# A CIN kernel on one core: block 1's first two tiles by plain transfers, the order of TensorE's first products, and the queues of the two output transfers

## The chip, the cores and the metric

The kernel runs on one core of a Trainium2 chip. The metric is the device time of one execution in microseconds (us). The core has five engines that run side by side and wait for each other by semaphores: TensorE (PE in the profile; its weight loads are PEld), VectorE (DVE), ScalarE (ACT), GpSimd (POOL) and SyncE (SP). Transfers are issued by SyncE, ScalarE or GpSimd, each with a queue of its own, and moved by the core's 16 DMA engines.

## What is computed

Three layers of a compressed interaction network for 1024 samples, each with 39 fields of 64 numbers, and a last linear layer on the sums of all three:

```python
def _cin_layer(Xk, X0, W, b):
    O = W.shape[0]
    Hk, Fdim = (Xk.shape[1], X0.shape[1])
    Wr = W.reshape(O, Hk, Fdim)
    return jnp.einsum('bhe,bfe,ohf->boe', Xk, X0, Wr) + b[None, :, None]
X0 = sparse_embedding            # 1024 x 39 x 64
Xk = X0
outs = []
for W, b in ((W0, b0), (W1, b1), (W2, b2)):   # 64 outputs each
    Xk = _cin_layer(Xk, X0, W, b)
    outs.append(Xk.sum(axis=-1))
cin_output = jnp.concatenate(outs, axis=-1)
return cin_output @ fc_w.T + fc_b
```

## The kernel before

**What it makes of the reference.** Layers 2 and 3 and the final layer are linear in their inputs apart from the products with X0, so the kernel folds W2, W1 and fc into a few small matrices during a preparation, and is left with the products of pairs of fields (layer 1's input) times weights, and one more multiplication per sample. The products of all pairs of 39 fields and a constant one are gathered in such a way that VectorE multiplies whole tiles of 128 rows, and TensorE multiplies the result by weights.

**Blocks and tiles.** The samples are cut into blocks of 32 (2048 columns). For a block, `rt` holds five tiles of 128 rows and 2048 columns of fp32 (8 KB a row). Each row is one field of the block, in an order that `label(i, row)` gives for tile i. `PAIRS` names six pairs of tiles; `product(n, c)` on VectorE is the product of one pair (the first one is tiles 0 and 1), and a seventh small one is made from `ut` and `vt`, for two blocks at a time. TensorE (`multiply`, L551) multiplies each product in four quarters of 512 columns. `rt` has two buffers: block 0 uses the first, block 1 the second.

**How the rows come.** The fields of a block are brought from the input into a table in DRAM, `xd`, with one row of 8 KB per field (`load`, L140), and are then spread over the 128 rows of each tile: `roll` issues one gather for each tile on GpSimd (L147), with row numbers from `lists`. Block 0's first four tiles are gathered in halves out of another table, `xh`, to be early. Later blocks (L719 and L763, most of the time) work in a different form, on tables `wc` and `wn`, with products made by L736.

**The preparation.** The names that matter here are: `fcrow2`, parts of fc doubled on GpSimd; `turn`, a product of one row that turns it into a column (L306); `spin`, fillers on TensorE that compute nothing of use (L259, into `idle`); V2, which is W2 with fc folded in (L386, then VectorE's transposes L406); `spread_v2` (L420, then VectorE's L433), which spreads it to both halves of the partitions; `turn_w0`, seven transposes of W0 (L399), read by ScalarE's copies L444; V1, which is W1 with V2 folded in (L467, then VectorE's transposes L480 and copies L487 and L490 into `both`); `weight_rows` (L508 and L510), which puts together the weights of one product in `pairs`; and `weight_turn`, which transposes them on TensorE (L527) and copies them into `wa` on ScalarE (L528). The order of the instructions on each engine is written out by hand.

**The order after that.** Block 0's first three products are made in halves, then the others; TensorE takes them in their order, block 0's seven, then block 1's six, and so on. VectorE makes a product four steps ahead of TensorE. On SyncE's queue stand, in order: fc's row, two copies of `xh` into `xd` (L376), the ones of the next table (L349), and the loads of blocks 2 and 3, and of 4 and 5. On GpSimd's queue stand block 0's gathers, u's and v's, block 1's five gathers, some small vectors, and then block 2's gathers.

**The end.** `finish_quarter` sums up the last block. Three rows of 256 results go out by SyncE (L1081), the last row by ScalarE (L1091); a last part of 8 results is made by VectorE (L1090).

Of the kernel before, what the change touches and what calls it, by code (L numbers as in the profile page):

```python
# [11 lines left out]
ALU = mybir.AluOpType  # L12
AX = mybir.AxisListType

B, F, E, H = 1024, 39, 64, 64
FH = F * H
FT = F + 1
# [3 lines left out]
NT = 5  # L21
# [8 lines left out]
MM = 512  # L30
# [9 lines left out]
NTAB = 3  # L40
NY = 3
# [19 lines left out]
def label(i, row):  # L61
    if row < K:
        return (row % F + BASE[i] + STEP[i] * (row // F)) % F
    e = row - K
    if i == NT - 1 and e < ONLY:
        return F
    return 3 * e + (e >= ONLY) + (e > ONLY) + OFFSET[i]


def small_labels(r):  # L70
# [44 lines left out]
def cin_kernel(ctx: ExitStack, tc: tile.TileContext, x, w0t, b0, w1, b1, w2, b2, fc_w, fc_b, out):  # L115
    nc = tc.nc
# [10 lines left out]
    xd = [dram.tile([2 * FT, BLK], F32, name=f"xd{k}") for k in range(NTAB)]  # L127
# [5 lines left out]
    def behind(work, product):  # L133
        if product is not None:
            info = mybir.DependencyInfo(mybir.DependencyClass.Sync, mybir.DependencyReason.DATA)
            tc.add_manual_dep(work.ins, product.ins.name, info, reason="one transfer per product")
# [15 lines left out]
    def tiles_of(n):  # L152
        return rt[(n + (n // 2 == NPART - 1)) % 2]

    def roll(n, tiles=range(NT), product=None):
        for i in tiles:
            k = n % 2 * NT + i
            gather_rows(tiles_of(n)[:, i], xd[n // 2 % NTAB][: FT if k < NT else 2 * FT], k, product)

    def roll_small(n):  # L160
        table = xd[n // 2 % NTAB].rearrange("f (t c) -> (f t) c", c=SUB)
        for k, dst in enumerate((ut, vt)):
            gather_rows(dst[n // 2 % 2], table, 2 * NT + k)
# [4 lines left out]
    v2v = v2.rearrange("p (low s b) -> p low s b", s=2, b=32)  # L168
# [18 lines left out]
    ones = const.tile([16, 2, 128], F32, name="ones")  # L187
# [3 lines left out]
    pairs = const.tile([128, NCHUNK, 128], F32, name="pairs")  # L191
    unit = const.tile([128, 128], F32, name="unit")

    def product(n, c, cols=slice(0, BLK), p=None):
        if p is None:
            p = prods.tile([128, BLK], F32, name="p", tag="p")
        if c < NPAIR:
            i, k = PAIRS[c]
            r = tiles_of(n)
            nc.vector.tensor_tensor(p[:, cols], r[:, i, cols], r[:, k, cols], ALU.mult)  # L200
        else:
            nc.vector.tensor_tensor(p[:, 0:SUB], ut[n // 2 % 2], vt[n // 2 % 2], ALU.mult)
        return p

    prep = tc.tile_pool(name="prep", bufs=1)
    with prep as prep:
# [5 lines left out]
        fcrow2 = prep.tile([1, 2, H, 2], F32, name="fcrow2")  # L212
# [8 lines left out]
        mask = prep.tile([128, 2], F32, name="mask")  # L221
# [31 lines left out]
        pw = [bank("pw") for _ in range(2)]  # L253
        small = bank("small")


        def spin(n=1, cols=MM // 2):
            for _ in range(n):
                nc.tensor.matmul(  # L259
                    idle[:, 0:cols],  # L260
                    nc.const_aps.tensor(1.0, (128, 128), F32),
                    nc.const_aps.tensor(1.0, (128, cols), F32),
                    start=True,
                    stop=True,
                )
# [23 lines left out]
        row, j, f0, late, v, extra = (new() for _ in range(6))  # L289
# [3 lines left out]
        for i in range(NT):  # L293
            at = OFFSET[i] - 3 * K + (0 if i < NT - 1 else -F)
            for k, by in enumerate((STEP[i], BASE[i], at)):
                nc.gpsimd.memset(shifts[:, k, i : i + 1], float(by))
        for k, by in enumerate((*SHIFT, ROWS, *(ROWS + by for by in SHIFT[NK - 1 :]))):
            nc.gpsimd.memset(shift_of[:, k : k + 1], float(by))
        one = ones[0:1, 0, 0:1]

        def double(dst, src):
            for s in range(2):
# [2 lines left out]
        def turn(dst, row):  # L305
            nc.tensor.matmul(dst, row, one, start=True, stop=True)  # L306
# [1 line left out]
        def turn_row(h, at, row, k):  # L308
            turn(small[h : h + H, at : at + 1], row[:, k * H : k * H + H])

        def turn_twice(at, row, k):
            turn(small[:, at : at + 1], row[:, k].rearrange("p h s -> p (h s)"))

        double(fcrow2[:, 1], fcrow[:, 2 * H : 3 * H])
        double(fcrow2[:, 0], fcrow[:, H : 2 * H])
# [4 lines left out]
        bothv = both.rearrange("p (a b) -> p a b", b=FT)  # L320
        nc.gpsimd.memset(bothv[0:H, :, F], 0.0)
        first = pw[1][:, MM - 1 : MM]
        turn(first, fcrow2[:, 1].rearrange("p h s -> p (h s)"))
        spin(1, MM // 4)

        nc.vector.tensor_copy(row, place)
        step(row, F, 1.0, j)
# [32 lines left out]
        r, most, far = (new() for _ in range(3))  # L360
# [22 lines left out]
        for k in range(2):  # L383
            for u in range(2):
# [5 lines left out]
                    start=True,  # L390
                    stop=True,
                )

        turn_twice(6, fcrow2, 0)
        spin(1, 3 * MM // 8)

        def turn_w0(k):
            n = min(128, NF * H - k * 128)
            nc.tensor.transpose(  # L399
                pw[k // 4][0:n, k % 4 * NW * F : (k % 4 + 1) * NW * F],  # L400
                w0s[:, k * 128 : k * 128 + n],
                unit[0 : NW * F, 0 : NW * F],
            )

        for k in range(2):
# [1 line left out]
                blocks[:, k].rearrange("p (f h) -> p f h", h=32),  # L407
                pv[k][:, 0:320].rearrange("p (h f) -> p f h", f=10),
            )
        nc.vector.tensor_scalar(v2v[:, 0, :, F - 32], mask, small[:, 6:7], None, ALU.mult)  # L410
        nc.vector.tensor_tensor(steps_at, steps_at, steps_by, ALU.mult)
        fused(seat, row, 96.0, seat, ALU.is_ge, ALU.add)
        step(row, 64.0, 2.0 * FT - 1.0, far)
# [4 lines left out]
        def spread_v2(u, lo, n):  # L418
            rows = slice(H * u, H * u + H)
            nc.tensor.matmul(  # L420
                pv[u][:, 0:n],
                twice[rows].rearrange("p h s -> p (h s)"),
                column[rows, lo : lo + n],
                start=True,
                stop=True,
            )

        spread_v2(0, 0, 20)
        spread_v2(1, 1, 19)
        for k in range(7):  # L430
            turn_w0(k)
        for u, at, low, lo, n in ((0, 0, 1, 0, 20), (1, 0, 1, 20, 12), (1, 12, 0, 0, 7)):
            nc.vector.tensor_tensor(  # L433
                v2v[:, low, :, lo : lo + n],
# [17 lines left out]
        nc.vector.tensor_tensor(both_of[:, 1:2], both_of[:, 0:1], jumps[:, 1:2], ALU.add)  # L452
        nc.vector.tensor_scalar(lists[:, 2 * NT :], both_of, 2.0, seat, ALU.mult, ALU.add)
        roll_small(0)
        roll(1)
        for h in (0, H):
            nc.gpsimd.dma_start(b0s[h : h + H], b0.rearrange("(h o) -> h o", o=1))
        nc.gpsimd.dma_start(b1s, b1.rearrange("(h o) -> h o", o=1).to_broadcast([H, 2]))
# [7 lines left out]
        for k, a in groups:  # L466
# [4 lines left out]
                start=True,  # L471
                stop=True,
# [2 lines left out]
        for h in (0, H):  # L475
            turn_row(h, 1, fcrow, 0)
        turn_row(0, 2, fcrow, 2)
        spin(3)
        for k, a in groups:
            nc.vector.transpose(  # L480
                flat[:, k], pt[k][:, 0 : 32 * NA].rearrange("p (h f) -> p f h", f=NA)
# [1 line left out]
        for k, a in groups:  # L483
# [4 lines left out]
            if k > 1:  # L488
                first = slice(0, 3) if k == 2 else slice(k, k + 1)
# [6 lines left out]
        first = [prods.tile([128, BLK], F32, name="p", tag="p") for _ in range(3)]  # L496


    def weight_rows(c, some=slice(None)):
        for at, n, a, b, sa, sb in RUNS[c][some]:  # L500
            out = pairs[:, c, at : at + n]

            def diagonal(p, q, sp, sq):
                at, by = p * FT + q, sp * FT + sq
                return both[:, at : at + by * (n - 1) + 1 : by]

            if b == F or a == b:
                nc.scalar.copy(out, diagonal(a, b, sa, sb))  # L508
            else:
                nc.vector.tensor_tensor(  # L510
                    out, diagonal(a, b, sa, sb), diagonal(b, a, sb, sa), ALU.add
                )
# [18 lines left out]
    work = ctx.enter_context(tc.tile_pool(name="work", bufs=2))  # L531
# [359 lines left out]
    steps = []  # L891
# [13 lines left out]
    p = {}  # L905
# [16 lines left out]
    for at, (n, c) in enumerate(steps[:3]):  # L922
        if at < 2:
            weight_rows(steps[3][1], slice(6 * at, 6 + 6 * at))
        product(n, c, halves[1], p[n, c])
    weight_rows(steps[4][1])
    n, c = steps[3]
    p[n, c] = product(n, c, halves[0])
# [149 lines left out]
            stop=True,  # L1078
        )
    nc.scalar.activation(y, py[0 : NY * 32, 0:YB], AF.Identity, bias=kfin)  # L1080
    nc.sync.dma_start(outv[0:NY], y[0 : NY * 32 : 32])  # L1081
    for lo, hi in ((0, done), (done, YB)):
        py = bank("py")[0:1, 0 : hi - lo]
        nc.tensor.matmul(
# [3 lines left out]
            nc.scalar.activation(yl[:, lo:hi], py, AF.Identity, bias=kfin[0:1])  # L1088
        else:
            nc.vector.tensor_scalar(yl[:, lo:hi], py, kfin[0:1], None, ALU.add)  # L1090
    nc.scalar.dma_start(outv[NY : NY + 1], yl)  # L1091


# [40 lines left out]
```

## Time and profile before

| | us |
|---|---|
| median of three runs | 735.3 |
| lowest and highest run | 733.25 and 736.11 |
| the profiled execution | 737.69 |
| its span, from first to last instruction | 735.9 |
| TensorE busy | 728.6 (99% of the span) |
| VectorE busy | 636.8 (87%) |
| GpSimd busy | 537.2 (73%) |
| ScalarE busy | 114.6 (16%) |

A row of the timeline or the waits names the engine, the line of the kernel, the operation, what it writes and reads, and how often; in brackets stand the idle time of the engine ahead of it and what ended that. SPq and ACTq are issues of transfers on those queues. The chain of waits follows the work that ended last back from the end, and gives for each piece its start, its length and its engine and line. A table by stretches gives for each engine the busy time within the stretch, and then the clock that TensorE was granted (1.00 is full), the mean busy share of the 16 DMA engines, and what they moved. The two tables of the busiest lines and of the slices are left out here.

### The profile page before, as it was taken

How to read it: one execution, taken by the hardware profiler on the slowest of the kernel's cores; microseconds unless marked ns; L12 is line 12 of the kernel's file. 1: busy time of each engine (PE TensorE's matmuls, PEld its weight loads, DVE VectorE, ACT ScalarE, POOL GpSimd, SP SyncE). 2: the span in 40 equal slices, each digit the busy share in tenths (PEclk: the TensorE clock that was granted, in tenths of full speed). 3: DMA queues.
4: the chain of work that ended last, by engine and by line, in shares of the span. 5: the costliest groups of instructions: out<-in, count | busy, mean ns of one | idle time of the engine just before them, and what ended most of it. 6: DMA issues, size and time to landing. Idle time of an engine off the chain costs nothing.

```text
span 735.9 us, 13756 instructions
## 1 busy us (share of the span) xinstructions
PE 728.6 (99%) x5930; PEld 339.0 (46%) x5930; DVE 636.8 (87%) x558; ACT 114.6 (16%) x198; POOL 537.2 (73%) x292
## 2 busy tenths in 40 slices
PE   8999999999999999999999999999999999999998
PEld 5444444444444444444444444444444444444443
DVE  6997999688897988979888897988979888897996
ACT  3242210020200202011020200202011020200322
POOL 7758988649778696987869778696987869775200
PEclk9999999999999999999999999999999999999999
DMA  9889998843938558284673937558294673855600
GB/s 299 306 262 411 374 293 254 260 153 96 319 94 250 195 159 293 68 299 141 201 245 93 321 94 253 193 157 289 70 301 142 206 240 95 288 175 190 268 1 0
DMA packets 77363, 153.56 MB, mean 209 GB/s; under 512 B 43848, under 2 KB 43917, under 8 KB 73974
## 3 DMA queue, kind: packets, MB, share of 16 engines
q0 software_dynamic: 32304, 130.39, 50.0%
q1 hardware_dynamic: 43298, 20.30, 11.3%
q10 hardware_dynamic: 1700, 1.99, 0.9%
q8 instruction: 46, 0.75, 0.4%
q14 instruction: 15, 0.12, 0.1%
HBM read 150.54 MB, written 10.60 MB: 219 GB/s over the span
## 4 chain that ended last, share of the span: by engine, by line
PE 98%; another core or an unknown queue 0%; issue 0%; DVE 0%; ACT 0%; DVEq 0%; ACTq 0%
PE po L763 76%; PE po L551 17%; PE po L776 2%; PE po L571 1%; PE idle L259 1%; PE po L582 0%; PE pv L386 0%; PE pw L399 0%; DVE flat L480 0%; ACT both L487 0%; PE tr L527 0%; DVE g L827 0%; PE po L691 0%; DVE sums L859 0%
## 5 line engine op out<-in xcount | busy, mean ns | idle before, releaser
L763 PE MATMUL po<-p,wc 32*128 32x512 f32 x1300 | 561.9, 588 | 0.0
L763 PE MATMUL po<-p,wn 32*128 32x512 f32 x3900 | 561.7, 588 | 0.0
L719 POOL DMA_INDIRECT r<-xd,narrow x130 | 381.0, 2931 | 99.0 <-DVE p L736 66.7
L763 PEld LDWEIGHTS po<-p,wn 32*128 32x128 f32 x3900 | 260.7, 185 | 209.8 <-issue 209.6
L763 PEld LDWEIGHTS po<-p,wc 32*128 32x128 f32 x1300 | 239.4, 185 | 86.6 <-issue 82.1
L736 DVE TENSOR_TENSOR p<-r 128x2048 f32<-128x2048 f32 x78 | 176.1, 2283 | 8.2 <-PE po L763 7.8
L825 ACT ACTIVATE z<-po,columns 64x512 f32<-64x512 f32 x128 | 87.3, 682 | 544.2 <-PE po L763 504.0
L736 DVE TENSOR_TENSOR p<-r,u 128x2048 f32<-128x2048 f32 x52 | 118.7, 2282 | 15.5 <-DMA r<-xd,narrow 8.0
L551 PE MATMUL po<-p,wa 128*128 128x512 f32 x288 | 127.5, 600 | 1.8 <-ACT wa L528 1.8
L200 DVE TENSOR_TENSOR p<-r 128x2048 f32<-128x2048 f32 (+2 forms) x42 | 82.1, 1978 | 8.2 <-DMA r<-xd,lists 5.1
L551 PEld LDWEIGHTS po<-p,wa 128*128 128x128 f32 x288 | 54.3, 192 | 70.8 <-issue 64.1
L147 POOL DMA_INDIRECT r<-xd,lists x26 | 67.5, 2594 | 25.9 <-DVE p L736 11.6
L736 DVE TENSOR_TENSOR p<-r,v 128x2048 f32<-128x2048 f32 x26 | 59.7, 2296 | 25.7 <-PE po L763 25.7
L827 DVE SCALAR_TENSOR_TENSOR g<-po,b0s,z 64x512 f32<-64x512 f32 x76 | 56.9, 749 | 5.7 <-ACT z L825 3.5
L719 POOL DMA_INDIRECT v<-xd,narrow x26 | 37.2, 1431 | 7.9 <-issue 7.9
L827 DVE SCALAR_TENSOR_TENSOR pairs<-po,b0s,z 64x512 f32<-64x512 f32 x26 | 19.5, 749 | 23.9 <-ACT z L825 21.7
L719 POOL DMA_INDIRECT u<-xd,narrow x26 | 27.5, 1057 | 7.9 <-issue 4.0
L809 DVE TENSOR_REDUCE sums<-g 103x16 f32<-103x1024 f32 x26 | 31.3, 1205 | 0.0
L827 DVE SCALAR_TENSOR_TENSOR both<-po,b0s,z 64x512 f32<-64x512 f32 x26 | 19.5, 749 | 0.8
L820 ACT COPY g<-r 39x1024 f32<-39x1024 f32 x12 | 12.1, 1042 | 31.9 <-DVE sums L848 18.9
L730 DVE TENSOR_TENSOR p<-u,v 128x1024 f32<-128x1024 f32 x13 | 15.7, 1209 | 1.1 <-PE po L763 1.1
L809 DVE TENSOR_REDUCE sums<-both 103x16 f32<-103x1024 f32 x13 | 15.7, 1205 | 0.0
(140 smaller groups left out, 184.4 us busy)
## 6 DMA issues: line engine op xcount, KB each, us to landing
xd<-in_x SPq DMA_DIRECT2D x30, 312.0 KB
g<-xd SPq DMA_DIRECT2D x26, 156.0 KB
r<-xd,narrow POOLq DMA_INDIRECT x130
pairs<-xd SPq DMA_DIRECT2D x13, 156.0 KB
both<-xd SPq DMA_DIRECT2D x13, 156.0 KB
wn<-wc SPq DMA_DIRECT2D x12, 168.0 KB
w2s<-in_w ACTq DMA_DIRECT2D x1, 624.0 KB
w1s<-in_w ACTq DMA_DIRECT2D x1, 624.0 KB
```

The source lines that it names most:

```text
L147: work = nc.gpsimd.indirect_dma_start(dst, None, table, bass.IndirectOffsetOnAxis(ap=lists[:, k : k + 1], axis=0))
L200: nc.vector.tensor_tensor(p[:, cols], r[:, i, cols], r[:, k, cols], ALU.mult)
L551: nc.tensor.matmul(po[n][m], wa[:, c, side : side + 2 * H], p[:, bass.ts(m, MM)], start=n % 2 == 0 and c == 0, stop=n % 2 == 1 and c == NP ...
L719: work = nc.gpsimd.indirect_dma_start(slot(k, j), None, table, bass.IndirectOffsetOnAxis(ap=narrow[:, j : j + 1], axis=0),)
L730: done = nc.vector.tensor_tensor(p[:, 0:SUB], slot(k, LEFT), slot(k, RIGHT + NK), ALU.mult)
L736: done = nc.vector.tensor_tensor(p.rearrange("p (k c) -> p k c", k=NK), slots(k, many, NK, side), slot(k, one)[:, bass.ts(side, MM)].unsqu ...
L763: nc.tensor.matmul(po[2 * k + side][s], weights(c, s)[:, kind : kind + 2 * H], p[rows, bass.ts(u, MM)], start=begin, stop=last and u == le ...
L776: nc.tensor.matmul(po[2 * k + side][s][half : half + H], weights(LINEAR, s)[:, H : 2 * H], slot(k, NK)[rows, bass.ts(side, MM)], start=Fal ...
L809: nc.vector.tensor_reduce(sums[:, at : at + BB].rearrange("p (h s b) -> p h s b", h=2, s=2)[:, :, side], g[k, side, b].rearrange("p (h b e ...
L820: nc.scalar.copy(gt[H : H + F], tiles_of(n)[0:F, 0, bass.ts(m, SUB)])
L825: nc.scalar.activation(z[one], po[n][m][other], AF.Identity, bias=fc0s[other])
L827: return lambda: nc.vector.scalar_tensor_tensor(gt[0:H, at], po[n][m][one], b0s[one], z[one], ALU.add, ALU.mult)
```

## The change

It has four parts.

Block 1's tiles 0 and 1 are no longer gathered by GpSimd. `stretches(i)` cuts a tile's 128 rows into stretches in which the table's rows follow at a fixed step, and `roll_plain` issues one plain transfer on SyncE's queue for each of these: for tile 0 of 39, 39, 39, 9 and 2 rows, for tile 1 of 4, 35, 2, 37, 39, 9 and 2 rows. They are made to wait for the second half of block 0's third product. The gathers of tiles 2 to 4 stay on GpSimd's queue.

fc's two light products (`turn`, L306) become `turn_wide`, with 128 columns of ones instead of one, so that the result stands 128 times side by side; both now stand ahead of V2. The fillers change with that: 128 columns ahead of V2 and 192 behind it become 64 ahead of it, and later three of 256 columns become two.

W0's seven turns stand ahead of V2's spreading instead of behind it.

At the end, the last row of results leaves by SyncE and the three others by ScalarE.

```diff
+def stretches(i):
+    found, row = [], 0
+    while row < 128:
+        first, n, by = label(i, row), 1, 0
+        if row + 1 < 128 and label(i, row + 1) >= first:
+            by = label(i, row + 1) - first
+            while row + n < 128 and label(i, row + n) - label(i, row + n - 1) == by:
+                n += 1
+        found.append((row, n, first, by))
+        row += n
+    return found
...
+    def roll_plain(n, i, product=None):
+        table = xd[n // 2 % NTAB][n % 2 * FT : n % 2 * FT + FT]
+        for row, many, first, by in stretches(i):
+            work = nc.sync.dma_start(
+                tiles_of(n)[row : row + many, i],
+                table[first : first + (many - 1) * by + 1 : max(by, 1)],
+            )
+            behind(work, product)
...
+            made[n, c] = nc.vector.tensor_tensor(
+                p[:, cols], r[:, i, cols], r[:, k, cols], ALU.mult
+            )
...
+        line = ones[0:1, 0, 0 : MM // 4]
...
-        def turn_twice(at, row, k):
-            turn(small[:, at : at + 1], row[:, k].rearrange("p h s -> p (h s)"))
+        def turn_wide(dst, k):
+            row = fcrow2[:, k].rearrange("p h s -> p (h s)")
+            nc.tensor.matmul(dst, row, line, start=True, stop=True)
...
-        turn(first, fcrow2[:, 1].rearrange("p h s -> p (h s)"))
-        spin(1, MM // 4)
+        turn_wide(pw[1][:, MM - MM // 4 : MM], 1)
+        second = small[:, MM - 1 : MM]
+        turn_wide(small[:, MM - MM // 4 : MM], 0)
+        spin(1, MM // 8)
...
-        turn_twice(6, fcrow2, 0)
-        spin(1, 3 * MM // 8)
-
...
-        nc.vector.tensor_scalar(v2v[:, 0, :, F - 32], mask, small[:, 6:7], None, ALU.mult)
+        nc.vector.tensor_scalar(v2v[:, 0, :, F - 32], mask, second, None, ALU.mult)
...
+        for k in range(7):
+            turn_w0(k)
         spread_v2(0, 0, 20)
         spread_v2(1, 1, 19)
-        for k in range(7):
-            turn_w0(k)
...
-        roll(1)
+        roll(1, range(2, NT))
...
-        spin(3)
+        spin(2)
...
         product(n, c, halves[1], p[n, c])
+    for i in range(2):
+        roll_plain(1, i, made[steps[2]])
     weight_rows(steps[4][1])
...
-    nc.sync.dma_start(outv[0:NY], y[0 : NY * 32 : 32])
...
-    nc.scalar.dma_start(outv[NY : NY + 1], yl)
+    nc.sync.dma_start(outv[NY : NY + 1], yl)
+    nc.scalar.dma_start(outv[0:NY], y[0 : NY * 32 : 32])
```

In the program, TensorE's first instructions stood in this order before, from the first light product to V1's products (pw, small, pv, pt and idle are banks of results; the brackets name the semaphores that an instruction waits for, DMAHW those of landed transfers):

```order
L306 MATMUL pw<-ones,fcrow_107 128x1 [waits DVE_49,Pool_49]
L259 MATMUL idle<-const-float32-1.0 128x128
L386 MATMUL pv<-w2s,fc_108 64x320 [waits DMAHW0_49,DVE_49]
L386 MATMUL pv<-w2s,fc_108 64x320 x3
L306 MATMUL small<-ones,fcrow_107 128x1 [waits Pool_49]
L259 MATMUL idle<-const-float32-1.0 128x192
L420 MATMUL pv<-blocks,twice 128x20 [waits DVE_49]
L420 MATMUL pv<-blocks,twice 128x19
L399 MATMUL pw<-unit,w0s 128x117 [waits DMAHW3_49]
L399 MATMUL pw<-unit,w0s 128x117 x5
L399 MATMUL pw<-unit,w0s 64x117
L467 MATMUL pt<-w1s,v_75 128x320 [waits DMAHW4_49,DVE_49]
```

Both light products now stand ahead of V2, and W0's turns, which wait for W0's transfer, between V2 and its spreading, as the same place of the changed program shows:

```order
L340 MATMUL pw<-ones,fcrow_107 128x128 [waits DVE_49,Pool_49]
L340 MATMUL small<-ones,fcrow_107 128x128 [waits Pool_49]
L285 MATMUL idle<-const-float32-1.0 128x64
L416 MATMUL pv<-w2s,fc_108 64x320 [waits DMAHW0_49,DVE_49]
L416 MATMUL pv<-w2s,fc_108 64x320 x3
L426 MATMUL pw<-unit,w0s 128x117 [waits DMAHW3_49,DVE_49]
L426 MATMUL pw<-unit,w0s 128x117 x5
L426 MATMUL pw<-unit,w0s 64x117
L447 MATMUL pv<-blocks,twice 128x20 [waits DVE_49]
L447 MATMUL pv<-blocks,twice 128x19
L494 MATMUL pt<-w1s,v_75 128x320 [waits DMAHW4_49,DVE_49]
```

W0's turns now also wait for VectorE, and the spreading is the last thing ahead of V1.

SyncE's queue read so before, from the copies of `xh` on (xd_68, xd_69 and xd_70 are the three tables):

```order
L376 DMA xd_68<-xh_72 39x1024 [waits DMAHW5_49]
L376 DMA xd_68<-xh_71 39x1024 [waits DMAHW2_49]
L349 DMA xd_69<-ones_95 16x2x128 [waits DMAHW0_49,Activation_49]
L140 DMA xd_69<-in_x 1248x1x64 [waits DMAHW1_49]
L140 DMA xd_69<-in_x 1248x1x64
```

The changed program has twelve transfers into block 1's tiles (r_89) between the copies and the ones; the last nine of them and what follows are:

```order
L176 DMA r_89<-xd_68 9x2048 [waits DMAHW3_49]
L176 DMA r_89<-xd_68 2x2048 [waits DMAHW4_49]
L176 DMA r_89<-xd_68 4x2048
L176 DMA r_89<-xd_68 35x2048 [waits DMAHW6_49]
L176 DMA r_89<-xd_68 2x2048 [waits DMAHW7_49]
L176 DMA r_89<-xd_68 37x2048 [waits DMAHW0_49]
L176 DMA r_89<-xd_68 39x2048 [waits DMAHW1_49]
L176 DMA r_89<-xd_68 9x2048 [waits DMAHW2_49]
L176 DMA r_89<-xd_68 2x2048 [waits DMAHW3_49]
L379 DMA xd_69<-ones_95 16x2x128 [waits DMAHW4_49,Activation_49]
L153 DMA xd_69<-in_x 1248x1x64 [waits DMAHW5_49]
L153 DMA xd_69<-in_x 1248x1x64 [waits DMAHW6_49]
```

Eight semaphores (DMAHW0 to 7) are used in turn, so that each transfer waits for the landing of the one eight places ahead; the ones and the loads of the next blocks now stand behind the twelve.

More of the change, by code (lines that the diff above doesn't have):

```diff
@@ L192, in cin_kernel @@
     unit = const.tile([128, 128], F32, name="unit")
+    made = {}
     def product(n, c, cols=slice(0, BLK), p=None):
@@ L199, in product @@
             r = tiles_of(n)
-            nc.vector.tensor_tensor(p[:, cols], r[:, i, cols], r[:, k, cols], ALU.mult)
+            made[n, c] = nc.vector.tensor_tensor(
+                p[:, cols], r[:, i, cols], r[:, k, cols], ALU.mult
+            )
         else:
```

## The prediction

> **What bounds the kernel now.** I read the chain of waits first, since it says which engine sets the end, then the busy time by stretches, then the timeline at the two places where the chain leaves TensorE or could be made to.
>
> ```profile
> PE 98%; another core or an unknown queue 0%; issue 0%; DVE 0%; ACT 0%; DVEq 0%; ACTq 0%
> core 0: us, PE busy (x) PEld busy (x) DVE busy (x) ACT busy (x) POOL busy (x), PEclk, DMA share, GB/s
> 0.00:20.00 20.00, 16.31 (x59) 10.99 (x59) 13.42 (x74) 6.92 (x17) 13.83 (x73) 0.99 0.91 306
> 20.00:46.00 26.00, 26.00 (x104) 11.14 (x105) 25.57 (x79) 9.05 (x34) 20.45 (x13) 0.94 0.84 313
> 123.00:686.00 563.00, 563.00 (x5304) 263.10 (x5296) 485.51 (x315) 68.17 (x100) 439.01 (x177) 1.00 0.60 197
> ```
>
> From 20 us on TensorE (PE) is busy in every microsecond of these stretches. The change doesn't touch those products, so it can gain only in the 20 us ahead of them and in the few at the end; it can lose wherever TensorE would have to wait. The start, piece by piece along the chain (start, length, what), is this:
>
> ```profile
> 5.34 2.33 PE pv L386 x8
> 7.67 0.51 PE small L306 x2
> 8.18 0.94 PE idle L259 x2
> 9.12 0.55 PE pv L420 x4
> 9.67 1.57 PE pw L399 x7
> ...
> 16.22 0.26 ACT pairs L508
> 16.48 3.08 another core or an unknown queue
> 19.56 0.25 ACT wa L528
> 19.81 0.04 issue
> 19.86 2.08 PE po L551 x2
> 21.93 0.21 PE tr L527
> 22.14 2.29 PE po L551 x4
> 24.43 0.11 PE tr L527
> 24.54 6.87 PE po L551 x16
> ...
> 45.89 39.68 PE po L551 x92
> ```
>
> The preparation ends at 19.86, when the first product's weights are there. Block 1's first product starts at 45.89: before it stand block 0's seven steps.
>
> **fc's light products, and W0's turns ahead of the spreading.** The two turns and their fillers before and behind V2 (0.51 and 0.94 in the chain, and as much ahead of it) become two 128-column turns and one short filler, all ahead of V2. What stands ahead of V2 keeps its length within a few tenths, so V2 still ends near 7.67. Then W0's turns can begin when W0 has arrived. No row shows the arrival: it lies before 9.67, where they start now. V1 follows: 1.57 for the turns, 0.55 for the spreading, and about 0.47 for VectorE's V2 and the hand-over (in the trace the spreading ends at 9.67 and VectorE's three pieces at 10.08).
>
> ```profile
> 9.71 0.37 DVE L433 TENSOR_TENSOR v<-pv,mask 128x40 f32<-128x40 f32 x3 [0.91 <-PE pv L420]
> 11.02 2.21 PE L467 MATMUL pt<-w1s,v 128*128 128x320 f32 x4
> 13.07 1.32 PE L467 MATMUL pv<-w1s,v 128*128 128x320 f32 x4
> ```
>
> V1 would start 2.59 us behind W0's first turn: at 10.26 if W0 is there at 7.67, at 12.26 if only at 9.67, against 11.02 now. That is a gain of 0.8 to a loss of 1.2; I take about 0, near the middle. The second gain is in V1's rate. The same four products take 2.21 us and then 1.32: TensorE speeds up at about 13, some 3.9 us into the work that runs without a hole from 9.12. After the change such a stretch runs from 0.78 to 7.67, so V1 should be at the fast rate from its start: 4 products less 0.22 each, 0.9 us. Of the start I expect 0.9 us, between a loss of 1.2 and a gain of 1.7.
>
> ```profile
> 17.28 0.30 PE L527 MATMUL tr<-unit,pairs 128*128 128x128 f32 x1 [1.07 <-issue]
> ```
>
> Of the three fillers one goes; TensorE idles 1.07 us behind them, so that shortens nothing. The turn they precede ends at 17.58, yet ScalarE reads it only at 19.56. The chain can't name what it waits for in the 3.08 us; I let them move with the rest.
>
> **The outputs swapped.** The last row's transfer moves to SyncE, the three rows to ScalarE.
>
> ```profile
> 0.73 0.36 SPq L230 DMA_DIRECT2D fcrow<-in_fc_w  x1
> 732.58 0.76 SPq L1081 DMA_DIRECT2D out_y<-y  x1
> 733.40 0.27 ACTq L1091 DMA_DIRECT2D out_y<-yl  x1
> ```
>
> A one-row issue costs SyncE 0.36 against ScalarE's 0.27; at most it costs 0.76, and the three rows leave earlier than the last one in both. Between no change and a loss of 0.5; I take 0.1.
>
> **Block 1's first two tiles on SyncE's queue.** POOL loses two of five gathers; SyncE gains twelve transfers. They wait for the third product's second half (the second of these two on VectorE, done at 26.78), and block 1's first product needs both tiles.
>
> ```profile
> 24.43 2.35 DVE L200 TENSOR_TENSOR p<-r 128x1024 f32<-128x1024 f32 x2
> 25.31 2.42 POOL L147 DMA_INDIRECT r<-xd,lists  x1 [0.30 <-issue]
> 28.04 4.88 POOL L147 DMA_INDIRECT r<-xd,lists  x1 [0.31 <-issue]
> ...
> 37.88 2.37 POOL L147 DMA_INDIRECT r<-xd,lists  x1 [0.30 <-issue]
> ...
> 37.15 2.29 DVE L200 TENSOR_TENSOR p<-r 128x2048 f32<-128x2048 f32 x1 [0.39 <-DMA r<-xd,lists]
> ```
>
> Today VectorE starts that product at 37.15, when the second tile lands, and ends at 39.44; TensorE wants it at 45.89. So there are 6.45 us of cover, and the tiles may land as late as 43.6. Will they? A plain transfer moves whole rows of 8 KB. How many of the 16 DMA engines share its rows is the question, and no transfer of 37 or 35 rows is in this trace. The nearest are SyncE's transfers of 39 rows. The view of the DMA queues gives packets, MB and the share of 16 engines; the first two rows are stretches in which SyncE's queue (q1) alone moved anything, in the middle of such transfers (172.4 to 173.4 and 437.9 to 438.5), the third is POOL's queue (q0) from 60 to 66, full of gathers:
>
> ```profile
> q1 hardware_dynamic: 107, 0.19, 82.1%
> q1 hardware_dynamic: 79, 0.14, 83.5%
> q0 software_dynamic: 338, 2.48, 97.9%
> ```
>
> SyncE's share stops at 82.1 and 83.5%, which is 13 engines of 16, and 39 is 13 times 3; a gather of 128 rows fills all. It looks as if rows are dealt in equal shares to a number of engines that divides their count. By this reading the second tile's stretch of 37 rows (a prime) goes to one engine. The third row gives an engine's rate: 2.48 MB in 6 us on 15.7 engines is 26.4 GB/s, 0.31 us for a row of 8 KB. If engines are taken from the first on, the first gets 3+3+3+1+1 rows of tile 0 and 1+5+1+37+3+1+1 of tile 1, together 60 rows or 18.6 us. In that time it also has eight rows of each of the three gathers that remain, 24 rows or 7.4 us, and the ends of u and v. The transfer of 37 rows is the ninth, and as there are eight counters of landings for these queues it waits until the first has landed; the rows ahead of it on its engine keep that engine busy meanwhile.
>
> Lower end: SyncE begins at about 25 (26.78 less what the start may gain), one issue takes 0.85 (two in the row below), the first engine serves SyncE alone: 25.9 and 18.6 give 44.5. Upper end: begin at 26.8, all gather rows in between: 27.7, 18.6, 7.4 and 2 for u and v give 55.7. If the rows went out evenly instead, the tiles would land by about 37, as now, and the edit would cost nothing: the twelve issues of at most 0.85 (10 us) are done before SyncE's next work, and POOL is freed earlier.
>
> ```profile
> 10.17 1.69 SPq L376 DMA_DIRECT2D xd<-xh  x2
> 39.15 0.35 SPq L349 DMA_DIRECT2D xd<-ones  x1
> 39.55 13.71 SPq L140 DMA_DIRECT2D xd<-in_x  x6
> ```
>
> Between these ends I take 53, since all three gathers are issued by about 40 and their rows can't be put off much longer. The first product is then ready at 53 plus 2.35, at 55.35: TensorE starts block 1 **9.5 us later** than at 45.89, whatever the start gained. After a pause TensorE is slow: behind the pause that ends at 19.86, two and four products of 0.43 each took 2.08 and 2.29 us, 1.8 more than at the later rate of 6.87 for 16. That again: **11.3 us**, and 0.1 for the output.
>
> What waits behind: SyncE's queue holds the loads of blocks 2 to 5 (39.55), whose share on that engine stands behind the rows; blocks 2 and 3 come later by some 4 us, but TensorE by 11.
>
> ```profile
> 62.56 2.29 DVE L200 TENSOR_TENSOR p<-r 128x2048 f32<-128x2048 f32 x1 [4.68 <-DMA r<-xd,lists]
> ```
>
> Block 2's first product ends at 64.85 today and is wanted at 66.5 (45.89 and 48 products of 0.43): 1.65 us of cover now, some 8 then. No second wait.
>
> Two rules of the Trainium skill bear on this. "DMA: Bandwidth & Descriptors", section "Why a DMA increments its semaphore by 16 and not by 1", says that a transfer from SyncE or ScalarE uses the largest number of engines up to 16 that divides the row counts; by it 37 rows go to one engine and 39 to 13. The 82.1 and 83.5% above agree; no run here has 37 rows. By it the sum is the 746.7 below, by an even deal 734.5. The same page, section "Queues, rings and completion order", lets each DMA engine take turns between queues, packet by packet; by it gather rows go in between and the landing is near the upper end, without it near the lower.
>
> **The sum.** The profiled execution took 737.69 us, of which the span is 735.9; the median of the runs shown is 735.3, which is 2.4 less. 737.69 and 11.4 give 749.1; on the scale of the median **746.7**.
>
> **The rivals.** (1) SyncE's rows are served first: landing at 44.5, product at 46.85, a loss of 1.0 and up to 0.9 of slow clock: 737.3. For it speaks that nothing shows how two queues share an engine; against it that the gathers fill the engines today. (2) The other side: the 37 rows are dealt evenly. Then the tiles land before 43.6, and only the start counts: 735.3 less 0.9 and plus 0.1, 734.5. It decides at a landing of 43.6. For it speaks that 13 engines can also be three rows each of 39 by rounding up, by which 37 rows would also take 13. (3) As (2), but the unnamed 3.08 us end at a time of their own, so that nothing is gained: 735.3. (4) As (2), but ScalarE reads the turn when it ends (2.0 less, from 19.56 to 17.58) and the clock stays up (1.8 less): 730.7.
>
> **How the numbers follow.** The forecast has 0.70, with 740 to 749.5 as its own range (landing at 48 to 55.7, with the slow clock whole or left out). Rival 1 has 0.07, rival 2 0.15, rival 3 0.05, rival 4 0.03. The range from 733.4 to 749.8 reaches to rivals 1 to 3. Half a per cent is 3.7 us, about what a measurement can tell: slower 0.70, same 0.27 (rivals 1 to 3), faster 0.03.
>
> **What would show it.** Right: VectorE's first product of block 1 waits for a SyncE transfer until 50 or later, TensorE pauses ahead of block 1 for some 10 us, the clock falls to 0.50 there, and the DMA share lies far below 1 in the last microseconds before. V1's parts at 0.33 each throughout would show the start's step right. Wrong: that product starts before 43.6, and TensorE runs on.

## The result, and the profile after

| | before | after |
|---|---|---|
| median of five runs each, us | 735.0 | 760.6 |
| lowest and highest | 733.25 and 736.11 | 758.94 and 761.39 |
| ratio, 95% interval | | 1.0338, 1.0317 to 1.0359 |
| span of the profiled execution | 735.9 | 758.9 |
| block 1's first product on TensorE starts | 45.89 | 67.39 |
| from there to the end of the span | 690.0 | 691.5 |

The change makes the kernel 3.4% slower, 25.7 us; forecast were 11.4. The two profiles differ by 23.0 us, and two places hold all of it: 21.5 us ahead of block 1, and 1.5 us behind that. The other 2.7 us between the medians lie in the profiled execution of before, which was 2.7 above its own median. In the experiments, one execution of the split (1287 us, at a mean clock of 0.56) is left out of the median.

The chain of waits of the changed kernel around that place (start, length, what):

```profile
25.68 0.33 SPq L176
...
27.98 20.38 DMA r<-xd
48.36 0.02 issue
48.38 16.43 DMA xd<-in_x
...
65.05 2.30 DVE p L224
67.35 0.04 issue
67.39 41.31 PE po L578 x92
```

SyncE begins with the twelve transfers at 25.68, VectorE starts on both tiles at 65.05, and TensorE starts block 1 when that product ends. The two waits stand in the timelines of VectorE and TensorE:

```profile
65.05 2.29 DVE L224 TENSOR_TENSOR p<-r 128x2048 f32<-128x2048 f32 x1 [28.77 <-DMA xd<-in_x]
67.39 12.99 PE L578 MATMUL po<-p,wa 128*128 128x512 f32 x26 [21.91 <-DVE p L224]
```

The chain and VectorE's row put the wait down to a load of `in_x`. The name is a guess by the time of landing; by the semaphore events of the trace, the 37 rows land at 62.96, the 39, 9 and 2 behind them at 63.89, 64.21 and 64.56, and the runs below show that it is those. Apart from one count about half a us behind each issue, the 37 rows land with a single count in these events, the 35 with seven, 39 rows with thirteen, 9 with nine and 2 with two. If each engine counts once, these are the numbers of engines that the prediction read out of its rows: equal shares, by a divisor of the number of rows.

The table by stretches (busy us of the five engines; then the granted clock, the share of the 16 DMA engines, GB/s) reads:

```profile
45.50:67.40 21.90, 0.01 (x1) 0.01 (x1) 2.35 (x3) 3.36 (x9) 0.80 (x1) 0.60 0.35 105
67.40:72.00 4.60, 4.60 (x7) 2.07 (x8) 4.57 (x19) 0.00 (x0) 3.99 (x3) 0.66 0.79 218
72.00:107.10 35.10, 35.10 (x83) 15.58 (x82) 34.75 (x43) 4.82 (x6) 23.48 (x15) 1.00 0.95 368
```

TensorE does nothing for 21.9 us, with a third of the DMA engines' time in use. The clock is at 0.66 for the first 4.6 us of block 1 and full from 72 on: that is the 1.5 us. What the DMA engines did meanwhile stands in the view of the queues, from 28 to 46 (first two rows) and from 53 to 62 (third row), again packets, MB and the share of 16 engines:

```profile
q0 software_dynamic: 436, 2.68, 63.0%
q1 hardware_dynamic: 261, 1.53, 35.1%
...
q1 hardware_dynamic: 81, 0.24, 6.7%
```

The third row is the single engine: 6.7% of 16 is 1.07 engines, and 0.24 MB in 9 us are 27 GB/s, the rate of one engine at 0.31 us a row. The first two rows are the surprise. The engines are full (98.1%, 15.7 engines), but move 4.21 MB in 18 us: 14.9 GB/s each, **0.55 us for a row of 8 KB**, where the gathers of the kernel before took 0.31. That holds for both queues: 14.8 GB/s an engine for the gathers (first row), 15.1 for SyncE's rows (second row).

### The profile page after: what moved, and what is told of

Same layout as the page of the kernel before. It is cut to its first block, busy times and chain, and to the rows that moved or that the text cites. A ratio compares the mean times of both kernels' runs of the same rounds, so it can differ in the third digit from the quotient of the medians.

```text
span 758.9 us, 13765 instructions
## 1 busy us (share of the span) xinstructions
PE 728.5 (96%) x5926; PEld 338.0 (45%) x5926; DVE 636.6 (84%) x558; ACT 114.8 (15%) x198; POOL 529.8 (70%) x290
## 4 chain that ended last, share of the span: by engine, by line
PE 92%; DMA 5%; DVE 2%; issue 0%; SPq 0%; ACT 0%; DVEq 0%
PE po L790 74%; PE po L578 14%; DMA r<-xd 3%; DMA xd<-in_x 2%; PE po L803 2%; DVE p L224 1%; PE idle L285 1%; PE po L598 1%; DVE pairs L537 0%; PE pv L416 0%; SPq L176 0%; PE po L609 0%; PE pt L494 0%; PE pv L494 0%; PE small L333 0%
## 5 line engine op out<-in xcount | busy, mean ns | idle before, releaser
L578 PE MATMUL po<-p,wa 128*128 128x512 f32 x288 | 129.1, 606 | 23.9 <-DVE p L224 21.9
L763 DVE TENSOR_TENSOR p<-r,u 128x2048 f32<-128x2048 f32 x52 | 118.7, 2282 | 16.2 <-PE po L790 11.6
L224 DVE TENSOR_TENSOR p<-r 128x2048 f32<-128x2048 f32 (+2 forms) x42 | 82.1, 1979 | 31.8 <-DMA xd<-in_x 28.8
L160 POOL DMA_INDIRECT r<-xd,lists x24 | 57.3, 2389 | 40.9 <-DMA xd<-in_x 22.6
L757 DVE TENSOR_TENSOR p<-u,v 128x1024 f32<-128x1024 f32 x13 | 15.7, 1211 | 1.1 <-PE po L790 1.1
L836 DVE TENSOR_REDUCE sums<-both 103x16 f32<-103x1024 f32 x13 | 15.7, 1206 | 0.0
```

Of the source, the lines that this page charges most:

```text
L160: work = nc.gpsimd.indirect_dma_start(dst, None, table, bass.IndirectOffsetOnAxis(ap=lists[:, k : k + 1], axis=0))
L224: made[n, c] = nc.vector.tensor_tensor(p[:, cols], r[:, i, cols], r[:, k, cols], ALU.mult)
L578: nc.tensor.matmul(po[n][m], wa[:, c, side : side + 2 * H], p[:, bass.ts(m, MM)], start=n % 2 == 0 and c == 0, stop=n % 2 == 1 and c == NP ...
L757: done = nc.vector.tensor_tensor(p[:, 0:SUB], slot(k, LEFT), slot(k, RIGHT + NK), ALU.mult)
L763: done = nc.vector.tensor_tensor(p.rearrange("p (k c) -> p k c", k=NK), slots(k, many, NK, side), slot(k, one)[:, bass.ts(side, MM)].unsqu ...
L836: nc.vector.tensor_reduce(sums[:, at : at + BB].rearrange("p (h s b) -> p h s b", h=2, s=2)[:, :, side], g[k, side, b].rearrange("p (h b e ...
```

## The experiments

Medians, and ratios to the kernel before on the same chip with their 95% intervals, stand with each run.

**Is it the 37 rows, and do they stand on one engine?** One run splits them, one puts 31 rows of the stretch of 35 beside them. Both edits are at this line; what they add is told behind the `#`:

```diff
         found.append((row, n, first, by))      # first run: n == 37 becomes 24 and 13
         found.append((row, n, first, by))      # second run: n == 35 becomes 31 and 4
```

> The changed kernel, with tile 1's stretch of 37 rows issued as two transfers of 24 and 13 rows. Theory A (37 rows on one DMA engine, and every row of 8 KB takes 0.5 to 0.6 us while SyncE's and POOL's queues share the engines, where the prediction had 0.31): no engine has more than about 26 of SyncE's rows, all engines have some 40 rows to move from 26 us on (five tiles of 128 rows over 16), 22 us at 0.55; both tiles land at 48 to 50, block 1's first product is ready at 50.5 to 52.5, TensorE restarts 5 to 7 us late instead of 21.5: 740 to 744 us. Theory B (one engine alone is the cause, a row takes 0.31 whoever shares the engine): landing near 41, no wait, 734 to 735. Theory C (what holds the product is the load of in_x that the chain of waits names from 48.38 to 64.81, or SyncE's eight counters): nothing changes, 760.

> The changed kernel, with tile 1's stretch of 35 rows issued as 31 and 4 rows; 31 is a prime, so by theories A and B these rows too stand on one engine, some 26 more rows there. If that is the engine on which the 37 rows stand, and these rows end up behind the gathers, where a row takes 0.31: 8 us more than the changed kernel, 768 to 770. If a row on a busy engine takes 0.55 and all of them count so: 775. If the single engine isn't the cause (theory C): 760.

Split: 750.4 us (1.0167 to 1.0226). With 31 rows: 768.6 us (1.0414 to 1.0477). The split takes away some 10 us and touches nothing but that stretch, so the load that the chain names isn't the cause (theory C falls), and 750.4 lies above both other theories. The second run costs 8 us more; on the first engine 5 rows become 32, and 27 rows by 0.31 are 8.4 us. In its semaphore events the 31 rows land as one at 59.07, and the 37 as one at 71.24. So 31 and 37 rows, prime numbers, do go to one engine each, and it is the same one; behind the gathers it moves a row in 0.31. The split has a profile of its own:

> The split of the 37 rows once more, for a profile: the first one was taken in an execution of 1287 us at a clock of 0.56. By the engine's count, 26 of SyncE's rows and 24 of the gathers' at 0.55 are 27.5 us from 26: landing at 53 to 54, TensorE restarting at 56 to 57, about 750.

```profile
53.94 2.29 DVE L228 TENSOR_TENSOR p<-r 128x2048 f32<-128x2048 f32 x1 [19.16 <-DMA xd<-ones]
```

Landing just ahead of 53.94, as 50 rows of 0.55 on one engine say (27.5 us from 26 on).

**Is it the plain transfers alone?** One run has them alone on the kernel before, the other everything but them (`roll(1)`, no `roll_plain`).

> The kernel before with the twelve plain transfers alone: fc's products, W0's turns and the outputs as before. If the plain transfers are the whole loss and the other parts gain about 1 at the start, which is covered by the wait: 760 to 762, TensorE restarting ahead of block 1 near 68. If part of the loss is the new order at the start: well under 760.

> The changed kernel with all five tiles of block 1 gathered by POOL, as before; the order of TensorE's first products and the outputs stay changed. The prediction's steps for these: 0.9 us gained at the start, 0.1 lost at the end, so 0.8 below the kernel before. The trace of the changed kernel has the third product's second half 1.1 us earlier; if all of this reaches the end: 1.0 below. If the start gains nothing: no difference. A loss: the new order is worse once the pause that hides it is gone.

761.2 us (1.0311 to 1.0373) and 735.2 us (0.9985 to 1.0012). The transfers are the whole loss. The rest of the change is worth nothing that shows: the interval reaches from 1.1 us gained to 0.9 lost, so the 1.0 and the 0.8 expected are not excluded, but not seen either.

**Are rows slow because the two queues share the engines?** Two runs hold the transfers back until the last gather has landed; this is the line that says what they wait for.

```diff
-        roll_plain(1, i, made[steps[2]])
+        roll_plain(1, i, landed[1, NT - 1])
```

> The changed kernel, with the twelve plain transfers waiting until the last of POOL's three gathers for block 1 (tile 4) has landed, near 39 us, instead of the third product at 25.7; 37 rows still on one engine. Theory A (a row takes 0.5 to 0.6 us only while two queues share an engine, 0.31 alone): the most loaded engine has 60 rows, 18.6 us, landing near 58 to 59, which is 6 us earlier than in the changed kernel although the transfers start 13 us later; TensorE restarts near 61, 750 to 755 us. Rival D (rows of plain transfers are slow by themselves, 0.5 to 0.6 us whatever the other queue does): 60 rows take 33 us, landing at 72, 768 us. Rival E (the start of the transfers is what counts, each row 0.31 and the tail the same): 13 us later than the changed kernel, 773 us.

> The late plain transfers, and the 37 rows split into 24 and 13. Theory A: the most loaded engine has 26 rows at 0.31, 8 us; from 39 to 40 the landing is at 48, the first product of block 1 ready near 50.5, 5 us late, with the slow clock 741 to 743 us: some 9 us better than the split alone (751), though the transfers start 13 us later. Rival D: 26 rows take 14 us, landing at 54, 748. Rival E: 13 us worse than the split alone.

762.3 us (1.0368 to 1.0414) and 751.9 us (1.0225 to 1.0283): theory A had 750 to 755 and 741 to 743, and falls. The view of the queues of the first of the two, from 40 to 48, when no gather was under way any more:

```profile
q1 hardware_dynamic: 228, 1.37, 74.8%
```

12.0 engines move 1.37 MB in 8 us, 14.3 GB/s each, 0.57 us a row: SyncE's rows are as slow alone as among gathers. That they start 13 us later costs only some 4 us by the ratios, since the gathers ahead then run undisturbed (3.67 MB at 89.3% of 16 engines from 28 to 38: 25.7 GB/s each, 0.32 a row). Rival D, which names no reason, is nearest (768 and 748). It misses by 6 in the first run because it prices all 60 rows of the first engine alike: 18 at 0.57 among SyncE's other rows and 42 at 0.31 alone are 23.3 us, and from SyncE's first issue (38.47) to VectorE's product (63.79) are 25.3.

**What makes a row slow?** Four runs fill block 1's tiles 0 and 1 by transfers whose numbers of rows 16 divides, so that every engine has 16 of SyncE's rows, with start and queue of the changed kernel; a fifth changes the partitions alone. These five fill the tiles with other rows than block 1 needs, so its results aren't the reference's; only times are read from them. The lines are shortened; each run has one of them, with the source that stands behind the `#`:

```diff
-        for row, many, first, by in stretches(i):
+        for row, many in ((0, 80), (80, 48)):      # source: the same table, then the input x
+        for row, many in ((0, 128),):              # source x
+        for row, many in ((0, 64), (64, 64)):      # source x
+        for k in range(2):                         # source x, into tile[k:128:2], 64 rows
```

> The changed kernel, with block 1's tiles 0 and 1 filled by transfers of 80 and 48 rows (numbers that 16 divides) taken one after the other from the same table, so that block 1's results are not the reference's; start and queue as in the changed kernel. All engines then have 16 of SyncE's rows and 24 of the gathers' at once. Theory A: 40 rows at 0.5 to 0.6, from 26 us on, the tiles landing between 44 (32 of them, alternating) and 48; first product ready at 46.5 to 50.5, 735 to 742 us, with packets of 0.5 to 0.6 us as long as both queues move. If rows take 0.31 once no engine is overloaded: landing by 38, 735 us, packets of 0.31.

> As the run before, but the 80 and 48 rows come from the input x, far from the table that the gathers read (block 1's results are again not the reference's). If the rows are slow because both queues read the same table: packets of 0.31 us, landing by 38, 735 us. If they are slow because two queues share an engine, whatever they read: as the run before, 0.5 to 0.6 us a row.

> As the run with rows of the input, but each of the two tiles in one transfer of 128 rows (block 1's results are again not the reference's). New theory F: a row is slow when the engines that run at once write into a narrow range of partitions, as transfers of 39, 48 or 80 rows do, whichever queue and table; an engine's 8 rows of a transfer of 128 would lie in a range of their own. By F packets are 0.31 us again, 40 rows an engine take 12.4 us from 26 to 27 on, landing by 41, little or no wait: 735 to 738 us. If plain transfers on SyncE's queue are slow as such: packets of 0.5 to 0.6, landing near 48, 743 us. The Trainium skill, "SBUF — State Buffer", section "Door 1: The DMA port swizzle", has a rule of that kind: 128 partitions lie behind 16 ports, and partitions 0 to 63 behind eight of them.

> As the run before, with the same rows and the same 16 engines, but each tile in two transfers of 64 rows, partitions 0 to 63 and then 64 to 127 (block 1's results are not the reference's). Theory F: 16 engines write into one half of the partitions at a time, packets of 0.5 to 0.6 us, landing at 46 to 48 and 742 to 744 us, as with 80 and 48 rows. If only a number that isn't a multiple of 16 or of 128 in rows per engine made the rows slow, or the source: packets of 0.31, 735 us.

> As the run with two transfers of 64 rows per tile, the same rows of the input over the same 16 engines, but written to the even partitions and then to the odd ones, so that each transfer reaches all 128 partitions' range (block 1's results are not the reference's). Theory F (the partitions that are written at once set the speed): rows of 0.31 us, landing by 41, 735 to 738 us. If the cut into 64 rows or their source were the cause: rows of 0.5 to 0.6, 742 to 745 us as with the two halves.

| rows, source, partitions | median us | interval of the ratio | first product of block 1 on VectorE | GB/s, 30 to 40 us |
|---|---|---|---|---|
| 80 and 48, same table, in order | 743.4 | 1.0108 to 1.0164 | 47.60 | 240 |
| 80 and 48, x, in order | 744.4 | 1.0094 to 1.0162 | 47.96 | 256 |
| 128, x | 736.3 | 0.9975 to 1.0013 | 40.38 | 421 |
| 64 and 64, x, lower and upper half | 744.6 | 1.0076 to 1.0141 | 49.09 | 242 |
| 64 and 64, x, even and odd | 735.1 | 0.9976 to 1.0023 | 39.71 | 418 |

The last column comes from the table by stretches, here of the last three runs in this order (the last two numbers of a row are the share of the DMA engines and GB/s):

```profile
30.00:40.00 10.00, 10.00 (x27) 4.49 (x27) 5.40 (x20) 3.28 (x20) 7.62 (x8) 1.00 1.01 421
```

```profile
30.00:40.00 10.00, 10.00 (x28) 4.54 (x27) 6.50 (x20) 2.89 (x18) 8.22 (x7) 1.00 1.03 242
```

```profile
30.00:40.00 10.00, 10.00 (x62) 4.25 (x68) 4.98 (x20) 4.98 (x20) 6.91 (x8) 1.00 1.01 418
```

The engines are full in all of them, and the rate is some 420, or 240 to 256 GB/s. Source and number of rows don't matter: the last two runs move the same 64 rows of x by 16 engines, first into one half of the partitions and then into the other, or into every second partition of all. Only the partitions written at once differ, and they make 242 or 418 GB/s and the whole loss of time: 1.0109 and 0.9999 of the kernel before, each on its own chip, which is some 8 us. (The two halves and the one transfer of 128 rows were run on the same chip: 8.3 us.) The gathers' rows beside them are slowed too. The gathers' queue alone, from 30 to 46 with the halves and from 29 to 38 with every second partition:

```profile
q0 software_dynamic: 255, 1.96, 52.9%
```

```profile
q0 software_dynamic: 271, 2.04, 55.0%
```

That is 14.5 and 25.8 GB/s an engine. By the Trainium skill, "SBUF — State Buffer", section "Door 1: The DMA port swizzle (why [64,N] ≈ [32,N])", transfers reach the 128 partitions through 16 ports, of which partitions 0 to 63 have eight; half of 418 is 209, and 242 with the gathers' rows among them is in keeping with that. The ports themselves no run shows; nor was a transfer of 39 rows on 13 engines run into spread partitions, so that its 0.55 has the same cause is inferred from these runs.

**Where did the start's gain go?** The kernel before got a second profile, and three runs issue ScalarE's copy of the ones, which SyncE waits for ahead of the loads of blocks 2 and 3, one or two steps earlier (`if at == NPAIR - 1` becomes `NPAIR - 2` or `NPAIR - 3`).

> The kernel before once more, for a second profile. In the first one block 0's first product starts at 19.86 and block 1's at 45.89; with the changed start and all tiles gathered these were 17.55 and 42.85, yet the times of the two kernels are the same. If the start of the kernel before varies from execution to execution, block 1 starts here at a time between 43 and 46; if it is always late, at 45.9, and the span is again near 735.9.

```profile
18.52 1.13 PE L551 MATMUL po<-p,wa 128*128 128x512 f32 x2 [0.82 <-ACT wa L528]
...
42.86 3.70 PE L551 MATMUL po<-p,wa 128*128 128x512 f32 x8
46.72 17.54 PE L551 MATMUL po<-p,wa 128*128 128x512 f32 x40 [0.16 <-DVE p L200]
66.56 3.67 PE L551 MATMUL po<-p,wa 128*128 128x512 f32 x8 [2.30 <-DVE p L200]
```

The same kernel, and block 1 starts 3.0 us earlier than in the first profile, yet the span is 736.0 again: TensorE waits 2.30 us for block 2's first product (and 0.16 within block 1) and is back at 66.56, where it was in the first profile without a wait. Here the 1.65 us of cover that the prediction counted are used up.

> The changed start and outputs, all tiles of block 1 gathered, and ScalarE's copy of the ones (which SyncE's queue waits for ahead of the loads of blocks 2 and 3) one step earlier. Theory G (block 2's tiles take back what the start gains): the loads begin near 33 instead of 37, block 2's first product no longer waits, and up to 2 to 3 us show that the two profiles differ by: 732 to 734 us. Rival H (the start's gain isn't there, or the loads collide with block 1's gathers and delay these as much): 735, no difference.

> As the run before, with that copy two steps earlier. Theory G: the loads begin near 30, among block 1's gathers; nothing more to gain for block 2, and block 1's gathers may lose 1 or 2 us of their 3 to 4 us of cover: 732 to 735 us. Rival H: 735 or slower.

> The kernel before with that copy one step earlier and nothing else. Theory G: what its own fast starts gain shows too; if the changed start is worth 0.9 us, this is 0.9 above the run with the changed start, 733 to 735 us. If both are the same, the changed start is worth nothing even with the cover gone. Rival H: 735.

734.0 us (0.9991 to 1.0022), 735.0 us (0.9995 to 1.0019) and 734.3 us (0.9994 to 1.0022): no difference. In the three profiled executions TensorE no longer waits for block 2; block 1 starts at 41.38, 44.24 and 41.22, and the span ends 690.1 to 690.2 us later, at 731.5, 734.4 and 731.3. So in a single execution an early start now reaches the end, but the medians don't follow. And the first and the third run, which differ in the start and the outputs alone, stand at 1.0007 and 1.0008: with the cover restored, too, the changed start is worth nothing that shows. What the profiles show instead is how far the start wanders. TensorE's first product in the profile of the third, which has the start of before:

```profile
14.47 1.13 PE L551 MATMUL po<-p,wa 128*128 128x512 f32 x2
```

With the start of before it begins at 19.86, 18.52, 18.59 (the plain transfers alone) and 14.47; in thirteen profiles with the changed one, those of the other experiments among them, between 14.68 and 19.42. One profile of each can't tell the two starts apart. Theory G is shown for single executions, not for the time; for the time, H's number holds, and which of its two reasons is left open. No kernel tried beats the one before.

## Why the prediction was wrong

**Right: the place and the mechanism.** The 37 rows go to one engine, both tiles are late, VectorE's first product of block 1 waits for SyncE's transfers, TensorE pauses ahead of block 1 (for 21.9 us, not some 10) with the clock at a mean of 0.60, and the DMA share lies far below 1 at the end. The sign was right, and rivals 2 to 4, in which the rows are dealt evenly, are excluded: the 37 rows land as one. So is rival 1: from 28 to 46 the gathers' queue moves 2.68 MB while SyncE's moves 1.53.

**Wrong: the landing, 53 where it was 64.56.** The step that failed is "0.31 us for a row of 8 KB", used for all rows on the first engine. The last 42 rows there (37, 3, 1 and 1), which the engine moved mostly alone, took 13.0 us at 0.31, so they began near 51.5. Ahead of them lie 25.9 us from 25.7 on, for 18 rows of SyncE's, 24 of the gathers' and the ends of u and v: 42 rows at 0.55 are 23.1 us, and 2.8 are left for u, v and the first issue, which the prediction had at 2.9. At 0.31 these 42 rows were 13.0: the price of a row is off by 10.1 us there, of the 11.6 that the landing is off. The rest is the choice of 53, 2.7 below the upper end, less the 1.1 by which the transfers began earlier than there. The upper end, 55.7, rested on the same 0.31 and so was no bound.

A warning stood in rows that the prediction itself quoted. SyncE's queue alone, 82.1% of 16 engines for 1 us, 0.19 MB: that is 13.1 engines at 14.5 GB/s each, about half the 26.4 of the gathers; the second row (0.14 MB in 0.6 us on 13.4 engines) gives 17. Their packets are of 2 KB, so they are no price for rows of 8 KB, and no run shows whether their low rate has the same cause; but they say that 26.4 can't be taken over unseen. The prediction took the number of engines from these rows and the rate from another one, of transfers that reach all 128 partitions.

**The slow clock.** 1.8 forecast, 1.5 measured (690.0 and 691.5 us behind block 1's start). The size was taken from the first products behind the pause at the start, the first two in 2.08 us. That isn't always so: of seventeen profiles three have 2.07 or 2.08 there, the others 1.12 to 1.42.

**The start.** V1's eight products take 2.58 us in the chain of the changed kernel, 0.32 each, near the forecast, though the first four are slower than the others:

```profile
10.30 1.42 PE pt L494 x4
11.72 1.16 PE pv L494 x4
```

V1 also starts 0.7 us earlier (10.30, 11.02 before), within the forecast's 0.8 gained to 1.2 lost. But no gain shows in the time: all tiles gathered, the rest of the change gives 0.9985 to 1.0012, at most 1.1 us gained. The step took one execution's start for the kernel's; with one order of instructions it wandered from 14.47 to 19.86. Block 2's first product can catch a part of what an early start gains, but with that wait out of the way no gain showed either.

**The outputs.** 0.1 forecast; with the start together no difference, and nothing smaller can be told.

**No second wait: right.** Block 2's gathers begin at 66.60 instead of 50.75, 16 us later where the prediction had about 4, but TensorE is 21.5 later; it waits for nothing else behind 67.39.

**The sum.** The measured 21.5 and 1.5 on the profiled 737.7 give 760.7, which is the profiled execution after (760.64) again: the two places hold the whole difference, and no further term is needed. That this execution is also the median of its five is chance. On the scale of the median, 2.4 lower as in the prediction, the same terms would end at 758.3, since the profiled execution of before was slower than its median and the one after was not.

## What to carry to other kernels

Before a gather is replaced by plain transfers, count for each transfer how many engines it gets (37 rows had one, 35 seven, 39 thirteen: the largest divisor up to 16) and which partitions are written at the same time: cutting the tiles into stretches was paid for twice here, with 0.55 us a row instead of 0.31 and with 37 rows on one engine. When a row of the queues' view is used, read share and MB together; the rate of an engine is in it. An end of a range that rests on a price from another kind of transfer is no bound, and one profile of a start that wanders says little about a gain of 1 us.

## What the hardware showed

- DMA engines that are full by their share can move half: 240 to 256 GB/s at a share of 1.01 to 1.03 into a part of the partitions, 420 GB/s at 1.01 into all, both with two queues at work. SyncE's rows alone, in stretches of up to 39, moved at 14.3 GB/s an engine on 12.0 engines, while one engine alone moved some 27.
- Transfers of one queue slow the rows of another on the same engines: with SyncE's transfers of 64 rows in halves, the gathers' queue moved 14.5 GB/s an engine, and 25.8 when every second partition was written.
- Plain transfers of 31 and 37 rows each landed as one, on one and the same engine; 35 rows landed in seven parts, 39 in thirteen.
- Four profiled executions with one and the same order at the start began the first product between 14.47 and 19.86 us; two of the very same kernel, 1.3 us apart there and 3.0 at block 1, had the same span within 0.1 us.
